# Block 0 of a two-layer transformer: two attention blocks to a group

## The chip, the cores and the metric

The kernel runs on one core of a Trainium2 chip. Its metric is the device time of one execution in microseconds (us); what is quoted is the median of several. A core has engines that run their own queues in program order and meet only at semaphores: TensorE (PE, with its weight loads PEld beside it), VectorE (DVE), ScalarE (ACT), GpSimd (POOL) and SyncE (SP), from whose queue the DMAs of this stage are issued.

## The reference

Two layers work on `x` (8 batches, 512 tokens, 256 channels), a condition (8, 256) and a context (8, 64, 192), all in fp32. The change touches only the first layer:

```python
mod = silu(c) @ adaln_w.T + adaln_b                  # nine rows of 256 per batch
shift_sa, scale_sa, gate_sa, shift_ca, scale_ca, gate_ca, shift_ff, scale_ff, gate_ff = split(mod, 9)
h = modulate(ln(x), shift_sa, scale_sa)              # ln(x) * (1 + scale) + shift
q = ln(heads(h)) * qn_w + qn_b                       # 16 heads of 16; q, k, v all from h
k = ln(heads(h)) * kn_w + kn_b
attn = softmax(q @ k.T * 16 ** -0.5)
x = x + gate_sa * unheads(attn @ heads(h))
h = modulate(ln(x), shift_ca, scale_ca)              # cross attention to 64 tokens
kv = brain_tokens @ cond_w.T + cond_b
...
x = x + gate_ca * (unheads(attn @ v) @ ca_out_w.T + ca_out_b)
h = modulate(ln(x), shift_ff, scale_ff)
x = x + gate_ff * ((silu(h @ w1.T) * (h @ w3.T)) @ w2.T)     # 1024 hidden
```

The second layer has self attention with rotary positions (16 heads of 64), cross attention to the normalized context, and a GELU feed-forward of 1024.

## The kernel before

The first layer is "block 0" of the kernel, the second "block 1". In block 0 each batch goes through three stages, written as the functions `batch1` (self attention), `batch2` (cross attention) and `batch3` (feed-forward).

**Slots and cycles.** The stages are laid out by hand on a row of slots. A cycle has 18 slots (`CYCLE = H + 2`). Sixteen of them hold the attention blocks of one batch in `batch1`: four groups `g` of four heads, by four key tiles `kt` of 128 tokens. Two more (`X0`, `X1`) hold the two blocks of the cross attention of the batch before. A block has two parts. Its scores are four matmuls of 16x512 that work in four row strips of the array and fill two PSUM tiles of two banks each (`bank_s`, of which there are just two); two exponentials of 128x1024 on ACT read them into `p`. Its values are four matmuls in four column strips, `p` against `h`, with a column of ones that gives the softmax denominators.

**What lies beside the slots.** `at(i, fn)` places any other work at slot `i`. `run_blocks` then emits everything: for each slot `i` the scores of block `i`, the values of block `i - 1`, and the work placed at `i`. The order on PE, DVE, ACT and POOL is this order of emission; no scheduler changes it. Cycles are counted from 0. From cycle 2 to cycle 7 three batches are in work: batch b in `batch1`, b-1 in `batch2`, b-2 in `batch3`. The placed work:

- of `batch1`: `norm` in three pieces (statistics of two tiles, of two more, then the layer norm into `ln`, and on POOL `ln` times the scale and plus the shift into `h`), `head_centre`, `head_var` (a square on ACT, a sum on DVE) and `head_scale` (a power and a product on POOL), which make the head norm in the tile `zx` (named `z` in the code); `queries_keys(g)`, four transposes of it, ACT for `q`, DVE for `k`; `group_end(g)`, which copies the values out to `oT`; `group_back(g)`, which transposes oT, divides by the denominators (`den`, `inv`, `attn` on DVE), and for the last group multiplies by the gate and adds to `x` on POOL, 128x1024 each.
- of `batch2`: `prepare(0..2)` (statistics twice, then the layer norm into `z` on DVE and, on POOL, the product `gb` and its addition to `x`), `turn` (eight transposes of `z` and two copies into `hT` on ACT), `queries`, the round trip of the denominators through DRAM (`inverse`, `scaled`), and `project_out` a cycle later.
- of `batch3`: `prepare(0..2)` and `turn` as above, `up(f)` for eight tiles of the hidden layer (four projections each, tanh on ACT, two products on DVE), `down(t)` for four token tiles (eight matmuls on `w_2` each); after every second one a product with the gate and an addition to `x` on DVE, 128x512 (`add_gated`).

PSUM besides the scores' four banks: one bank for values (`ps_O`), and three that `bank_x()` hands out in turn (`ps_X`, `ps_D`) to transposes and projections.

All of the matmuls and transposes but some are issued by helpers, so most PE rows carry one line of the code (109); the tiles' names tell them apart. `ps_S<-q,k` are scores, `ps_O<-p,h` values, `ps_X` or `ps_D<-hT,w` the up projections, `<-w,hid` the down projections, `<-ident,...` transposes, `<-p,vb` and `<-p,sel` the cross attention's values and denominators.

Of the kernel before, what the change touches and what calls it, by code (L numbers as in the profile page):

```python
# [18 lines left out]
P = 128  # L19
# [3 lines left out]
DX = D + HD0  # L23
NPAIR = H // 2
# [19 lines left out]
class Block:  # L44


    def __init__(self, scores, values):
        self.scores, self.values = scores, values
        self.before, self.after = [], []


def run_blocks(blocks, beside=None):


    beside = dict(beside or {})
    for fn in beside.pop(-1, []):
        fn()
    early, late = {}, {}
    for i, bl in enumerate(blocks):
        for lead, fn in bl.before:  # L60
            early.setdefault(max(i - lead, 0), []).append(fn)
        for lag, fn in bl.after:
            late.setdefault(i + 1 + lag, []).append(fn)
    i = 0
    while i <= len(blocks) or any(k >= i for k in (*late, *beside)):
        for fn in early.get(i, []):
            fn()
        if i < len(blocks):
            for fn in blocks[i].scores:
                fn()  # L70
        if 1 <= i <= len(blocks):
            for fn in blocks[i - 1].values:
                fn()
        for fn in (*late.get(i, []), *beside.get(i, [])):
            fn()
        i += 1


def fast_path(ctx: ExitStack, tc: tile.TileContext, a: dict, out: bass.AP):
# [150 lines left out]

    sp_stack = ExitStack()
# [56 lines left out]
    nc.gpsimd.memset(hs[0][:, :, :, HD0 : HD0 + 1], 1.0)  # L288
    nc.gpsimd.memset(sc32, 0.0)
# [189 lines left out]
    X0, X1 = 9, 13  # L479


    def batch1(b):
# [8 lines left out]
        def norm(n):  # L491

            if n == 0:
                s["bc"] = bc = wk.tile([P, 3 * D], F32, tag="bc", name="bc")
                s["h"] = hs[b % 2]
                s["hv"] = s["h"][:, :, :, 0:HD0]
                s["ln"] = wk.tile([P, NT, D], F32, tag="ln", name="ln", bufs=1)
                s["pieces"] = norm_pieces(lambda: s["ln"], xs[b], EPS0)
                if b:
                    spread(bc, b, SH_SA, 3 * D)  # L500
            s["pieces"][n]()
            if b and n == 2:
                ln, bc = s["ln"], s["bc"]
                nc.gpsimd.tensor_tensor(ln, ln, bc[:, None, D : 2 * D].to_broadcast([P, NT, D]), ALU.mult)
                shift = bc[:, 0:D].rearrange("p (h d) -> p h d", d=HD0)
                nc.gpsimd.tensor_tensor(s["hv"], ln.rearrange("p t (h d) -> p t h d", d=HD0),
                                        shift[:, None].to_broadcast([P, NT, H, HD0]), ALU.add)
# [11 lines left out]
        def head_rows():  # L519
            s["z"] = wk.tile([P, NT, DX], F32, tag="zx", name="zx", bufs=1)  # L520
            nc.gpsimd.memset(s["z"][:, :, D if b else 0 : DX], 0.0)

        def head_centre(c, par=None):

            hv = s["hv"][:, :, 8 * c : 8 * c + 8] if par is None else s["hv"][:, :, 8 * c + par : 8 * c + 8 : 2]
            sh = [P, NT, hv.shape[2]]
            mean = small.tile(sh, F32, tag=f"mean{sh[2]}", name="mean", bufs=2)
            nc.vector.tensor_reduce(mean, hv, AX.X, ALU.add)
            nc.vector.tensor_scalar_mul(mean, mean, 1.0 / HD0)
            nc.vector.tensor_tensor(parts(s["z"][:, :, 0:D], c, par), hv,  # L530
                                    mean[:, :, :, None].to_broadcast([*sh, HD0]), ALU.subtract)

        def head_var(c, par=None):
            sq, z = parts(s["ln"], c, par), parts(s["z"][:, :, 0:D], c, par)
            sh = [P, NT, z.shape[2]]
            nc.scalar.activation(sq, z, AF.Square)
            s["var", c, par] = var = small.tile(sh, F32, tag=f"var{sh[2]}", name="var", bufs=2)
            nc.vector.tensor_reduce(var, sq, AX.X, ALU.add)
            nc.vector.tensor_scalar(var, var, 1.0 / HD0, EPS0, ALU.mult, ALU.add)

        def head_scale(c, par=None, eng=None):
            var, z = s["var", c, par], parts(s["z"][:, :, 0:D], c, par)
            n = z.shape[2]
            half = mhalf[:, 0 : NT * n].rearrange("p (t h) -> p t h", t=NT)
            nc.gpsimd.tensor_tensor(var, var, half, ALU.pow)  # L545
            (eng or nc.gpsimd).tensor_tensor(z, z, var[:, :, :, None].to_broadcast([P, NT, n, HD0]), ALU.mult)

        def queries_keys(g):
# [3 lines left out]
            lo = c * P + par * HD0  # L552
            for t in range(NT):
                nc.tensor.transpose(ps[:, t * P : (t + 1) * P], s["z"][:, t, lo : lo + P], ident)  # L554
# [6 lines left out]
        def block(g, kt):  # L561
# [4 lines left out]
            def score():  # L566
# [5 lines left out]
                for u in range(2):  # L572
                    pr[u] = wk.tile([P, 2, N], F32, tag="p", name="p", bufs=4)
                    nc.scalar.activation(pr[u], pss[u], AF.Exp, scale=HD0 ** -0.5)  # L574
# [10 lines left out]
        def group_end(g):  # L585
            oT = wk.tile([P, N], F32, tag="oT", name="oT")
            nc.scalar.copy(oT, s["o", g])  # L587
            s["oT", g] = oT

        def group_back(g):  # L590
            c, par = divmod(g, 2)
            if g == 0:
                s["attn"] = wk.tile([P, NT, D], F32, tag="tok", name="attn", bufs=1)
# [3 lines left out]
            o = s["attn"][:, :, c * P : (c + 1) * P].rearrange("p t (j e d) -> p t j e d", j=4, e=2)[:, :, :, par, :]  # L597
# [5 lines left out]
            nc.vector.tensor_tensor(o, i[:, :, :, 0:HD0], inv[:, :, :, None].to_broadcast([P, NT, 4, HD0]), ALU.mult)  # L603
            check(inv.rearrange("p t j -> p (t j)"))
            if g == 3:
                at_, x = s["attn"], xs[b]
                gate = s["bc"][:, None, 2 * D : 3 * D].to_broadcast([P, NT, D])
                nc.gpsimd.tensor_tensor(at_, at_, gate, ALU.mult)
                nc.gpsimd.tensor_tensor(x, x, at_, ALU.add)

        n = 0
        for g in range(4):
            for kt in range(NT):
# [4 lines left out]
                if g == 0 and kt == 0:  # L618
                    if b == 0:
                        def before():  # L620
                            head_rows()
# [3 lines left out]
                            first_modulated(0, 0)  # L625
                            head_centre(0, 0)
                            head_var(0, 0)
                            head_scale(0, 0, nc.vector)

                        def gate():  # L630
                            spread(s["bc"][:, 2 * D : 3 * D], b, G_SA, D)
# [3 lines left out]
                        at(0, lambda: first_modulated(0, 1))  # L635
                        at(0, lambda: head_centre(0, 1))
                        at(1, lambda: head_var(0, 1))
                        at(1, lambda: head_scale(0, 1))
                        at(2, lambda: first_modulated(1))
                        at(3, lambda: head_centre(1))  # L640
                        at(4, lambda: head_var(1))
                        at(4, lambda: head_scale(1))
                        at(5, gate)
                    else:
                        for m in range(3):
                            at(i - 11 + m, lambda m=m: norm(m))
                        at(i - 6, head_rows)
                        for c in range(2):
                            at(i - 6, lambda c=c: head_centre(c))
                            at(i - 5, lambda c=c: head_var(c))  # L650
                            at(i - 4, lambda c=c: head_scale(c))
                if kt == 0:
                    at(i - 2, lambda g=g: queries_keys(g))
                if kt == NT - 1:
                    at(i + 1, lambda g=g: group_end(g))
                    at(i + 2, lambda g=g: group_back(g))
# [3 lines left out]
    def batch2(b):  # L660
# [27 lines left out]
        def block(c):  # L688
            def score():
# [4 lines left out]
                for u in range(2):  # L694
                    s["p", c, u] = p = wk.tile([P, 2, N], F32, tag="p", name="p", bufs=4)
# [35 lines left out]
        for n in range(3):  # L731
            at(base + 3 + n, lambda n=n: prepare(n))
# [12 lines left out]
    def batch3(b):  # L745
        s = {}

        base = CYCLE * (b + 2) + (3 if b in (B - 3, B - 2) else -2 if b == B - 1 else 0)
# [28 lines left out]
        def down(t):  # L777
            qp, j = divmod(t, 2)
            if j == 0:
                s["ps"] = bank_x()  # L780
            project_tile(s["ps"], j, lambda k: s["hid"][:, k, :], w_2, 8, t)
            if j == 1:
                add_gated(wk2, b, s["gate"])(qp, s["ps"].rearrange("p (j d) -> p j d", j=2))

        for n, i in enumerate((5, 5, 5) if b == B - 1 else (4, 5, 7)):
            at(base + i, lambda n=n: prepare(n))
        later.append((base + 7, turn))
        for f in range(8):
            at(base + 8 + f, lambda f=f: up(f))
        for t in range(4):  # L790
            at(base + 16 + t, lambda t=t: down(t))
# [19 lines left out]
    for t, i in enumerate((10, 11, 14, 15)):  # L811
# [38 lines left out]
    def keys1(p):  # L850
# [3 lines left out]
        kv1[p] = q = kv1["pool"].tile([P, N], F32, tag="q", name="q", bufs=5)  # L854
# [46 lines left out]
    at(CYCLE, open_cross)  # L901
    for p in range(NPAIR):
        at(CYCLE + 4 + p, lambda p=p: keys1(p))
        at(CYCLE + 8 + p, lambda p=p: store_keys1(p))
# [1335 lines left out]
```

## Time and profile before

| what | value |
|---|---|
| time, median of 3 runs | 2450.28 us (2448.86 to 2451.66) |
| time of the profiled execution | 2448.82 us |
| its span, first to last instruction | 2446.9 us |
| granted TensorE clock, mean | 0.997 |
| in one steady cycle (447.8–545.5 us): 32 exponentials of `batch1` on ACT (L574) | 31.0 us |
| there: 48 + 16 up projection matmuls (`ps_X`, `ps_D` <- hT,w) on PE | 22.3 + 7.7 us |
| there: two powers of the head norm (L545) on POOL | 10.9 us |
| whole run: DMA | 84.07 MB, mean 34 GB/s |

The span is the time between the first and the last instruction of one profiled execution; 1.92 us of that execution lie outside it. A row of the timeline has the start in us, the length in us, the engine, the line of the kernel, the operation, the tiles written and read, the shapes and the number of instructions put together in the row; in square brackets the idle time before it and what ended it. In the windows view each row has the window, its length, and for each engine the busy time with the number of instructions in parentheses, then the granted clock, the busy share of the DMA engines and GB/s. The lengths of matmuls are modelled, so where a step's price is wanted it is read from start to start.

### The profile page before, as it was taken

The numbers are of one execution on the slowest core, as the hardware profiler recorded it, in microseconds if no ns is written. First come the engines' busy times: TensorE is split into PE (matmuls) and PEld (weight loads), VectorE is DVE, ScalarE is ACT, GpSimd is POOL, SyncE is SP. The second block draws the span as 40 slices with busy tenths as digits, with TensorE's granted clock in tenths as the row PEclk, the third lists the DMA queues.
The fourth block names the chain that finished last, engine by engine and source line by source line (L and its number), as shares of the span: only waits on it lengthen the run. The fifth ranks groups of instructions, "written<-read, shape, count | busy, mean of one in ns | idle before, by whom it ended". The sixth has DMA issues, their size and how long they took to land.

```text
span 2446.9 us, 28449 instructions
## 1 busy us (share of the span) xinstructions
PE 2408.0 (98%) x10964; PEld 1157.3 (47%) x10964; DVE 1058.9 (43%) x2083; ACT 878.5 (36%) x1118; POOL 858.5 (35%) x538
## 2 busy tenths in 40 slices
PE   9999999999998999999999999999999999999999
PEld 4333443444435643444444444434345555566665
DVE  5544435434434434343434343434334766651210
ACT  4565545545452123333333333333332221222221
POOL 3443222222301026343434343434333444531110
PEclk9999999999999999999999999999999999999999
DMA  5120000000001000000000000000123222210000
GB/s 181 45 93 7 16 20 8 17 11 12 13 11 64 27 1 23 18 19 19 19 18 19 18 19 19 19 18 19 36 61 96 68 67 67 64 55 27 22 18 23
DMA packets 84400, 84.07 MB, mean 34 GB/s; under 512 B 42544, under 2 KB 58784, under 8 KB 84256
## 3 DMA queue, kind: packets, MB, share of 16 engines
q1 hardware_dynamic: 83352, 81.09, 10.6%
q8 instruction: 88, 1.44, 0.2%
q10 hardware_dynamic: 904, 1.07, 0.1%
q14 instruction: 56, 0.46, 0.1%
HBM read 72.09 MB, written 10.04 MB: 34 GB/s over the span
## 4 chain that ended last, share of the span: by engine, by line
PE 92%; DVE 3%; issue 1%; ACT 1%; DMA 1%; POOL 1%; SPq 0%; POOLq 0%; DVEq 0%; ACTq 0%
PE ps_X L109 38%; PE ps_S L109 23%; PE ps_O L109 14%; PE ps_D L109 14%; PE ps_X L416 1%; DVE t L836 1%; DMA rec<-rec 1%; DMA rb<-rec 1%; POOL p L1252 1%; ACT p L574 0%; PE ps_X L554 0%; PE ps_X L596 0%; PE ps_D L416 0%; DVE t L833 0%; ACT hT L417 0%
## 5 line engine op out<-in xcount | busy, mean ns | idle before, releaser
L109 PE MATMUL ps_S<-q,k 32*128 32x512 f32 (+1 forms) x3072 | 429.1, 625 | 7.3 <-ACT p L574 3.1
L1012 ACT ACTIVATE p<-ps_S 128x1024 f32<-128x1024 f32 x256 | 248.1, 1022 | 522.1 <-PE ps_S L109 522.1
L574 ACT ACTIVATE p<-ps_S 128x1024 f32<-128x1024 f32 x256 | 248.2, 1021 | 232.1 <-PE ps_S L109 230.7
L109 PEld LDWEIGHTS ps_S<-q,k 32*128 32x128 f32 (+1 forms) x3072 | 160.5, 184 | 233.1 <-issue 137.5
L991 DVE TENSOR_TENSOR t<-ps_X,rope_c 128x512 f32<-128x512 f32 x126 | 87.2, 692 | 349.9 <-PE ps_X L109 349.9
L1031 DVE TENSOR_TENSOR sm<-sm,p 128x1024 f32<-128x1024 f32 x128 | 190.6, 1532 | 59.2 <-ACT p L1012 59.2
L994 POOL TENSOR_TENSOR q<-t 128x512 f32<-128x512 f32 x32 | 40.8, 1276 | 406.6 <-DVE t L992 406.6
L175 POOL TENSOR_TENSOR rstd<-rstd,mhalf 128x4 f32<-128x4 f32 x49 | 51.0, 1042 | 326.8 <-DVE rstd L174 325.2
L1027 POOL TENSOR_TENSOR sm<-p 128x1024 f32<-128x1024 f32 x64 | 149.3, 2354 | 38.0 <-ACT p L1012 38.0
L109 PE MATMUL ps_X<-hT,w 128*128 128x512 f32 x344 | 160.5, 601 | 1.3 <-ACT hT L417 0.9
L837 POOL TENSOR_TENSOR q<-t,t 128x512 f32<-128x512 f32 x72 | 95.1, 1321 | 176.4 <-DVE t L836 172.4
L109 PE MATMUL ps_O<-p,h 128*32 128x512 f32 x1024 | 139.4, 614 | 1.6 <-ACT oT L587 1.6
L109 PE MATMUL ps_O<-p,v 128*64 128x512 f32 x512 | 138.0, 617 | 0.0
L109 PE MATMUL ps_D<-p,v 128*64 128x512 f32 x512 | 131.6, 592 | 0.0
L453 DVE TENSOR_TENSOR x<-ps_X,x 128x512 f32<-128x512 f32 x27 | 18.7, 692 | 239.4 <-PE ps_X L109 239.4
L109 PE MATMUL ps_X<-hT,w_sa_wq 128*128 128x512 f32 x256 | 115.9, 595 | 3.0 <-ACT hT L417 3.0
L109 PE MATMUL ps_X<-w_sa_wv,hT 128*128 128x512 f32 x256 | 118.0, 604 | 0.0
L109 PE MATMUL ps_X<-w_sa_wo,oT 128*128 128x256 f32 x512 | 114.5, 382 | 0.1
L545 POOL TENSOR_TENSOR var<-var,mhalf 128x32 f32<-128x32 f32 (+1 forms) x17 | 87.3, 5135 | 75.2 <-ACT t L773 41.7
L109 PE MATMUL ps_X<-hT,w_sa_wk 128*128 128x512 f32 x248 | 112.4, 596 | 0.0
L109 PE MATMUL ps_S<-hT,w_ff_w 128*128 128x512 f32 x256 | 111.3, 592 | 0.0
L109 PEld LDWEIGHTS ps_X<-w_sa_wo,oT 128*128 128x128 f32 x512 | 96.0, 190 | 24.2 <-issue 11.4
(282 smaller groups left out, 3537.0 us busy)
## 6 DMA issues: line engine op xcount, KB each, us to landing
rb<-rec SPq DMA_DIRECT2D x128, 128.0 KB
rb<-rec_d SPq DMA_DIRECT2D x124, 128.0 KB
rb<-rec SPq DMA_DIRECT2D x16, 256.0 KB
out_dram<-x SPq DMA_DIRECT2D x15, 256.0 KB
x<-in_x_dram SPq DMA_DIRECT2D x7, 512.0 KB
bc<-modd SPq DMA_DIRECT2D x7, 384.0 KB
gate<-modd SPq DMA_DIRECT2D x16, 128.0 KB
k_d<-q SPq DMA_DIRECT2D x8, 256.0 KB
```

What stands on the lines that cost most here:

```text
L109: nc.tensor.matmul(o, lhsT, rhs, start=start, stop=stop)
L175: nc.gpsimd.tensor_tensor(r[:, :n], r[:, :n], mhalf[:, :n], ALU.pow)
L416: nc.tensor.transpose(ps[:, t * P : (t + 1) * P], z[:, t, k * P : (k + 1) * P], ident)
L545: nc.gpsimd.tensor_tensor(var, var, half, ALU.pow)
L574: nc.scalar.activation(pr[u], pss[u], AF.Exp, scale=HD0 ** -0.5)
L836: nc.vector.tensor_tensor(t2[d], ps[src], sn[src].to_broadcast([64, *shape[1:]]), ALU.mult)
L837: nc.gpsimd.tensor_tensor(dst, t1, t2, ALU.add)
L991: nc.vector.tensor_tensor(c, ps, rope_c, ALU.mult)
L994: nc.gpsimd.tensor_tensor(r[0], ec, os, ALU.subtract)
L1012: nc.scalar.activation(pr, pss[u], AF.Exp, scale=HD1 ** -0.5)
L1027: nc.gpsimd.tensor_tensor(sm, s["p", g, 0, u], s["p", g, 1, u], ALU.add)
L1031: nc.vector.tensor_tensor(s["sm", g, u], s["sm", g, u], s["p", g, t, u], ALU.add)
```

## The change

- `run_blocks` goes by groups of two: for odd `i` the scores of block `i`, the work placed at `i-2` and `i-1`, the scores of block `i+1`, then the values of blocks `i-1` and `i`. So that the cross attention's blocks fall into one group, `X0` goes from slot 9 to 11. The exponential buffers `p` go from four to six, `oT` from two to one.
- The head norm's tile becomes two standing tiles `zs[0]` and `zs[1]`, one for each half of the heads, zeroed once at the start; `head_rows` with its memset per batch is gone. The square is a piece of its own, `head_square`.
- The modulation rows `bc` lose the gate, which gets its own tile and DMA.
- `group_back` multiplies by the gate and adds to `x` for each of the four groups, 128x256 each, in place of one 128x1024 pair for each batch.
- `down(t)` has a half bank, a product and an addition of its own for each `t`, 128x256.
- The placed work moves: `norm` from slots 11, 10, 9 before the batch's first block to 15, 14, 13 before; the head norm's pieces to 11, 9, 7, 7 before for the first half and four later for the second; `queries_keys` from two slots ahead of its group to four (for the group at slot 4 two); `prepare` of `batch2` from 3, 4, 5 to 3, 3, 5; `batch3` by the table `places`, in most batches with `down` at every second slot; some of cycle 0's and cycle 1's setup work by one to four slots.

```diff
-def run_blocks(blocks, beside=None):
...
-    while i <= len(blocks) or any(k >= i for k in (*late, *beside)):
...
-            for fn in blocks[i].scores:
+def run_blocks(blocks, beside):
     for fn in beside.pop(-1, []):
         fn()
+    top = max(len(blocks) + 2, *(k + 3 for k in beside))
+    for i in range(-1, top, 2):
+        for k in (i, i + 1):
+            for fn in blocks[k].scores if 0 <= k < len(blocks) else []:
                 fn()
-        if 1 <= i <= len(blocks):
-            for fn in blocks[i - 1].values:
+            if k == i:
+                for fn in (*beside.get(i - 2, []), *beside.get(i - 1, [])):
+                    fn()
+        for k in (i - 1, i):
+            for fn in blocks[k].values if 0 <= k < len(blocks) else []:
                 fn()
-        for fn in (*late.get(i, []), *beside.get(i, [])):
-            fn()
-        i += 1
...
+    zs = [wk.tile([P, NT, DZ], F32, name=f"z{c}", bufs=1) for c in range(2)]
...
-    X0, X1 = 9, 13
+    X0, X1 = 11, 13
...
-                s["bc"] = bc = wk.tile([P, 3 * D], F32, tag="bc", name="bc")
+                s["gate"] = wk.tile([P, D], F32, tag="gate", name="gate")
...
-                    spread(bc, b, SH_SA, 3 * D)
+                    s["bc"] = bc = wk.tile([P, 2 * D], F32, tag="bc", name="bc", bufs=1)
+                    spread(bc, b, SH_SA, 2 * D)
+                    spread(s["gate"], b, G_SA, D)
...
-        def head_rows():
-            s["z"] = wk.tile([P, NT, DX], F32, tag="zx", name="zx", bufs=1)
-            nc.gpsimd.memset(s["z"][:, :, D if b else 0 : DX], 0.0)
...
+        def head_square(c, par=None):
+            nc.scalar.activation(parts(s["ln"], c, par), head_z(c, par), AF.Square)
...
-                    pr[u] = wk.tile([P, 2, N], F32, tag="p", name="p", bufs=4)
+                    pr[u] = wk.tile([P, 2, N], F32, tag="p", name="p", bufs=6)
...
-            if g == 3:
-                at_, x = s["attn"], xs[b]
-                gate = s["bc"][:, None, 2 * D : 3 * D].to_broadcast([P, NT, D])
-                nc.gpsimd.tensor_tensor(at_, at_, gate, ALU.mult)
-                nc.gpsimd.tensor_tensor(x, x, at_, ALU.add)
+            nc.gpsimd.tensor_tensor(attn, attn, gate.to_broadcast([P, NT, 4, HD0]), ALU.mult)
+            nc.gpsimd.tensor_tensor(x, x, attn, ALU.add)
...
-                        for m in range(3):
-                            at(i - 11 + m, lambda m=m: norm(m))
-                        at(i - 6, head_rows)
+                        for m, k in enumerate((-15, -14, -13)):
+                            at(i + k, lambda m=m: norm(m))
                         for c in range(2):
-                            at(i - 6, lambda c=c: head_centre(c))
-                            at(i - 5, lambda c=c: head_var(c))
-                            at(i - 4, lambda c=c: head_scale(c))
+                            for k, fn in ((-11, head_centre), (-9, head_square), (-7, head_var), (-7, head_scale)):
+                                at(i + k + 4 * c, lambda c=c, fn=fn: fn(c))
                 if kt == 0:
-                    at(i - 2, lambda g=g: queries_keys(g))
+                    at(i - (2 if i == 4 else 4), lambda g=g: queries_keys(g))
                 if kt == NT - 1:
                     at(i + 1, lambda g=g: group_end(g))
-                    at(i + 2, lambda g=g: group_back(g))
+                    at(i + 2 + (n + 1) % 2, lambda g=g: group_back(g))
...
-        for n in range(3):
-            at(base + 3 + n, lambda n=n: prepare(n))
+        for n, i in enumerate((3, 3, 5)):
+            at(base + i, lambda n=n: prepare(n))
         at(base + 6, turn)
...
-        base = CYCLE * (b + 2) + (3 if b in (B - 3, B - 2) else -2 if b == B - 1 else 0)
+        base = CYCLE * (b + 2) + {B - 3: 4, B - 2: 3, B - 1: -2}.get(b, 0)
...
         def down(t):
-            qp, j = divmod(t, 2)
-            if j == 0:
-                s["ps"] = bank_x()
-            project_tile(s["ps"], j, lambda k: s["hid"][:, k, :], w_2, 8, t)
-            if j == 1:
-                add_gated(wk2, b, s["gate"])(qp, s["ps"].rearrange("p (j d) -> p j d", j=2))
+            ps = bank_x()[:, 0:D]
+            project_tile(ps, 0, lambda k: s["hid"][:, k, :], w_2, 8, t)
+            tmp = wk2.tile([P, 2, D], F32, tag="tmp", name="tmp", bufs=1)[:, 0, :]
+            nc.vector.tensor_tensor(tmp, ps, s["gate"], ALU.mult)
+            x = xs[b][:, t, :]
+            nc.vector.tensor_tensor(x, x, tmp, ALU.add)
...
-        for n, i in enumerate((5, 5, 5) if b == B - 1 else (4, 5, 7)):
-            at(base + i, lambda n=n: prepare(n))
-        later.append((base + 7, turn))
+        places = {B - 2: (3, 3, 5, 6, 9), B - 1: (5, 5, 5, 7, 8)}.get(b, (4, 4, 7, 8, 9))
+        for n in range(3):
+            at(base + places[n], lambda n=n: prepare(n))
+        later.append((base + places[3], turn))
         for f in range(8):
-            at(base + 8 + f, lambda f=f: up(f))
+            at(base + places[4] + f, lambda f=f: up(f))
         for t in range(4):
-            at(base + 16 + t, lambda t=t: down(t))
+            at(base + places[4] + 8 + (t if b > B - 3 else 2 * t), lambda t=t: down(t))
```

`spread` issues one DMA from SP's queue that copies modulation rows from DRAM to all partitions; `project_tile` and `project_out` run the matmuls of a projection for one token tile or for two.

## The prediction

> **What bounds the kernel now.** I read the page's busy shares first, then the chain of waits.
>
> ```profile
> PE 2408.0 (98%) x10964; PEld 1157.3 (47%) x10964; DVE 1058.9 (43%) x2083; ACT 878.5 (36%) x1118; POOL 858.5 (35%) x538
> PE 92%; DVE 3%; issue 1%; ACT 1%; DMA 1%; POOL 1%; SPq 0%; POOLq 0%; DVEq 0%; ACTq 0%
> ```
>
> TensorE is never short of work for long: a gain must come out of its own sequence, a loss from anything that makes its queue stand. All edits lie in block 0, which the PE timeline shows at 19–857 us. From one cycle's first scores to the next's it takes 65.9, 72.1 and 95.25 us in cycles 0 to 2, 97.66 in each of 3 to 6, and 120.6 in cycle 7 with its tail. The windows view of one steady cycle, and of a stretch used later:
>
> ```profile
> 447.80:545.50 97.70, 97.40 (x509) 42.62 (x508) 43.76 (x107) 50.08 (x62) 28.76 (x14) 1.00 0.05 14
> 757.00:762.00 5.00, 4.93 (x13) 2.74 (x14) 1.85 (x8) 1.56 (x2) 2.35 (x1) 0.66 0.00 0
> ```
>
> (Length; busy PE, weight loads, DVE, ACT, POOL; granted clock; DMA share.) PE idles 0.3 us of 97.7, yet DVE is busy less than half.
>
> **What grouping gives.** The PE timeline:
>
> ```profile
> 600.79 1.14 PE L109 MATMUL ps_S<-q,k 16*128 16x512 f32 x8
> 601.86 1.06 PE L109 MATMUL ps_O<-p,h 128*32 128x512 f32 x8
> 602.86 1.98 PE L109 MATMUL ps_D<-hT,w 128*128 128x512 f32 x4
> 604.68 1.88 PE L109 MATMUL ps_X<-hT,w 128*128 128x512 f32 x4
> 606.49 1.14 PE L109 MATMUL ps_S<-q,k 16*128 16x512 f32 x8
> ...
> 619.35 1.06 PE L109 MATMUL ps_X<-p,vb 128*32 128x512 f32 x8
> 620.23 1.04 PE L109 MATMUL ps_X<-p,sel 128*32 128x512 f32 x8
> 621.20 0.66 PE L596 MATMUL ps_D<-ident,oT 128*128 128x128 f32 x4
> ```
>
> Start to start, scores take 1.07, values 1.00, a projection pair 3.63. In the middle of a run, eight projection matmuls start 0.427 apart, 3.413 in all; four scores in parallel rows, or four values in parallel columns, are two such passes, 0.853. So leaving scores costs 0.218, values 0.143, projections 0.217. Values behind values (619.35 to 621.20) take 1.85 for 1.707: the change of shape is paid once, 0.147. Two slots paid 2×(0.218+0.143+0.217) = 1.156; a group of scores, beside, scores, two values pays 2×0.218+0.217+0.147 = 0.80, 0.36 less. A steady cycle: 97.66 = 32.4 (18 slots' scores and values) + 6.51 (their exits) + 53.56 (projections and transposes) + 16×0.217 + 1.70 (stalls). After: 32.4 + 53.56 + 18×0.218 + 9×0.147 + 9×0.217 = 93.2.
>
> One stall is new. A block needs both score tiles; its two exponentials start 1.24 us after its scores and take 1.94, so the second tile is free some 3.2 after. Scores that follow two values come 1.07+1.85 = 2.92 after the last ones: 0.29 in 7 of 9 groups. Steady cycle 95.2, −2.45.
>
> **What the new places cost.** Take the group that holds the work of slots 5 and 6, from t7, the transpose of oT behind the scores of slot 7. PE goes on with down(3) on w_2 (3.41), then eight transposes of batch2's z (0.9), and would be at the next scores at t7+4.75. Before, `prepare(2)` wrote z at slot 5, and slot 6's scores and values ran before `turn`; now both are in one group, and in DVE's order z stands behind the multiply and add that need the end of down(3). DVE comes late besides: norm (slots 3, 4, 5), both statistics of `prepare` (3, 3) and `down` are packed into two groups. From t5, the start of down(2) (t7 = t5+8.34), with the DVE timeline's durations:
> - down(2) ends, tmp and x (0.4 each, from attn's 0.42 of the same size): t5+4.4
> - the statistics ending `prepare`: two pairs of 0.75+0.30, overlapped, and rstd, 1.78: 6.2
> - k 0.81, norm's statistics 0.9, `prepare` of batch2 1.78, waits between: t5+10.3 = t7+1.96
> - den, inv, attn, chk 1.1; ln apply 1.4; tmp and x 0.8; z 1.38: t7+6.7.
>
> The last transpose would end at t7+7.05, a wait of 2.3. That is the lower bound, DVE being as fast as it is alone. The POOL and DVE timelines say that it isn't:
>
> ```profile
> 459.72 2.36 POOL L609 TENSOR_TENSOR x<-x,attn 128x1024 f32<-128x1024 f32 x1
> ...
> 478.15 2.37 POOL L437 TENSOR_TENSOR x<-x,gb 128x1024 f32<-128x1024 f32 x1
> ```
>
> ```profile
> 460.48 2.15 DVE L462 TENSOR_TENSOR x<-x,tmp 128x512 f32<-128x512 f32 x1
> ...
> 463.45 0.69 DVE L462 TENSOR_TENSOR x<-x,tmp 128x512 f32<-128x512 f32 x1
> ...
> 476.09 1.38 DVE L208 TENSOR_SCALAR z<-x,mv,rstd 128x256 f32<-128x256 f32 x4
> ...
> 479.42 2.21 DVE L208 TENSOR_SCALAR z<-x,mv,rstd 128x256 f32<-128x256 f32 x4
> ```
>
> The same add is 0.69 alone and 2.15 when it meets a POOL add, and then ends 0.55 after it; z is 1.38 alone, 2.21 beside L437. DVE operations that read PSUM, and statistics, keep their times. In this group POOL now has five operations: attn·gate and x+attn (0.73 each, from the 128x256 gb of L675), ln·scale and h (2.36 each, L504 and L506), gb 0.73. The ln apply, the add and z are held: ln·scale runs from about t7+5.5 to 7.9, the add slips in, h ends at 10.6, one piece of z, gb until 11.4, the rest of z, the transposes: t7+12.75. The wait is 12.75−4.75 = 8.0. Only one more collision, with L437's 2.37, lies above: 10.4. I take 8.0, because the held rows are these very operations. Queued behind: z's transposes on PE, hence the scores of slot 8, their exponentials on ACT, the whole cycle.
>
> Such a wait has a second price:
>
> ```profile
> 757.06 1.44 PE L416 MATMUL ps_D<-ident,z 128*128 128x128 f32 x4 [4.53 <-DVE z L208]
> ```
>
> Behind it, the window 757–762 has clock 0.66, that is 3.41 us at one half, 1.7 lost. I add 1.7 to a wait of 8, nothing to one of 2.3. The Trainium skill's page TensorE: Matmul & The Clock Gate (Part 1, What's actually happening) has the clock halve after an idle window of about 3.4 us and recover after a busy one, the windows running free; by that a wait of 8 could cost 1.7 to 3.4, up to 7 more over four cycles than the sum here.
>
> **Cycle by cycle.**
> - Cycle 0: eight groups at 0.36, less a few 0.29, −2.2. The gaps beyond the exits come to 8.2 today; I let half go, −4.1 (none or all: ±4). But `queries_keys(2)`, at slot 4, now transposes its z in the group in which that z is still squared, summed, raised and scaled; the POOL timeline:
>
> ```profile
> 37.56 5.43 POOL L545 TENSOR_TENSOR var<-var,mhalf 128x32 f32<-128x32 f32 x1 [8.00 <-DVE var L539]
> ```
>
> Exponentials 3.2, square 0.6, var 0.9, power 5.43, product 1.06 (L546) = 11.2, less 1.7 of PE work ahead: 9.5. With the clock's 1.7: +5.
> - Cycle 1: −2.1, a wait of 6 (fewer statistics), clock 1.7: +5.6.
> - Cycle 2: −2.6, short groups +0.9, wait 8, clock 1.7: +8.
> - Cycles 3–6: 4×(−2.45+8.0+1.7) = +29.
> - Cycle 7, without norm: a wait of 1.9, −2.45: −0.5. Tail: the 4.53 falls to 2.4 (−2.1) and its clock loss goes (−1.7), the waits view's 1.2, 1.1 and 0.9 go (−3.1), block 1's first norm now stands before the last hid on DVE (+2.9): −4.
>
> At nothing: the standing z tiles (a 0.15 us memset per batch saved on POOL, idle 65%); exponential buffers, oT, q of kv1 (their users lie slots apart); the adds of `group_back` (5.8 us per batch on POOL for 4.7, beside TensorE; where they meet DVE they are in the 8.0); bc's 384 KB as 256+128, one more issue of 0.32 on SP's queue, now ahead of the softmax round trips: bc is read some 13 us later, and nothing waits for bc today. Were that cover gone, its lateness would move h and add to the same wait.
>
> Sum: 5+5.6+8+29−0.5−4 = +43. The profiled run took 2448.82 (span 2446.9 and 1.9 around it), 1.5 under the median: 2448.8+43 = 2492; I say 2490.
>
> **Rivals.**
> - *The vector chain alone*: POOL's and DVE's pieces interleave without holding each other. For: half of DVE's work here is untouched by POOL today. Against: 460.48, 479.42. Wait 2.3, full clock: cycles 3–6 −0.6, 0 +5, 1 and 2 +0.8, end −4.5: 2449.5. Chance 0.14.
> - *Faster: DVE is in time.* If the statistics fill DVE's waits for down(2) and down(3), z starts right behind down(3)'s add, and PE waits for tmp, x and a first piece, 1.2. Cycles 3–6: 4×(1.2−2.45) = −5; 1 and 2 −1.4; 0 −2, if its z is done some 6 us sooner; end −5.3: 2435. It decides where z begins by t7+5; against it, my 6.7 even without collisions. Chance 0.24: my order of pieces may be off by microseconds.
> - *Pairs save nothing*: exponentials hold the second scores by 0.36 more a pair, so −2.2, −2.1, −2.6 and 5×−2.45 fall away: 2490+19 = 2509. Against it, ACT at 50 of 97.7. Chance 0.05.
>
> **Numbers.** Forecast 0.57, own range 2470 (waits of about 4, no clock loss) to 2506 (10.4). For 8 in 10: 2437 to 2508. A measurement tells 0.2%, 4.9 us, from none: faster 0.22, same 0.10, slower 0.68.
>
> **What would show it.** Right: in each of cycles 2–6 a gap of 6–10 us before transposes of batch2's z, released by DVE's z, clock below 1 behind it, cycles of 103–106; two values in 1.85; some scores 0.3 late. Wrong: cycles below 96 with PE idle under 2, or a gap that DVE's z doesn't end.

## The result and the profile after

The changed kernel takes 2526.8 us (median of 6 runs, 2524.31 to 2529.75) against 2450.2 before: ratio 1.0319, 95% interval 1.0309 to 1.0329. The forecast had the sign; its range for 8 in 10 (2437 to 2508) ended 19 us too low. The page of the changed kernel, busy times and chain:

```profile
PE 2437.1 (96%) x10964; PEld 1185.6 (47%) x10964; DVE 1093.0 (43%) x2115; ACT 880.9 (35%) x1118; POOL 866.4 (34%) x580
PE 88%; DVE 5%; issue 2%; POOL 2%; ACT 1%; DMA 1%; SPq 1%; ACTq 0%; DVEq 0%; POOLq 0%
```

PE has the same 10964 instructions, but span less busy time is 90.4 us instead of 38.9: 51 us more of idleness. And it is busy for 29.1 us longer with the same work, although pairs of blocks were to shorten it: the work ran slower. The windows view, cycles 0 to 2 and one steady cycle (length; busy PE, weight loads, DVE, ACT, POOL; granted clock; DMA share):

```profile
18.90:110.40 91.50, 71.90 (x351) 24.80 (x352) 35.62 (x97) 38.98 (x45) 32.02 (x20) 0.74 0.23 71
110.40:192.50 82.10, 75.05 (x395) 26.86 (x394) 44.03 (x91) 43.27 (x52) 35.38 (x24) 0.88 0.20 63
192.50:296.00 103.50, 94.43 (x440) 35.46 (x440) 47.38 (x109) 51.17 (x63) 35.32 (x22) 0.87 0.11 35
404.20:509.70 105.50, 99.00 (x508) 45.97 (x505) 48.93 (x111) 50.69 (x63) 29.68 (x19) 0.95 0.04 13
```

| stretch | length before, after (us) | change | forecast | PE idle before, after | clock before, after |
|---|---|---|---|---|---|
| cycle 0 | 65.9, 91.5 | +25.6 | +5 | 5.5, 19.6 | 0.97, 0.74 |
| cycle 1 | 72.1, 82.1 | +10.0 | +5.6 | 3.3, 7.1 | 1.00, 0.88 |
| cycle 2 | 95.3, 103.6 | +8.3 | +8 | 0.3, 9.1 | 0.95, 0.87 |
| cycles 3 to 6 | 4 x 97.66, 105.3 to 105.7 | +31.4 | +29 | 0.3, 6.5 each | 1.00, 0.95 |
| cycle 7 and tail, to block 1's first scores | 238.3, 243.0 | +4.7 | -4.5 | 8.4, 7.0 | 0.99, 0.99 |

Idle is a window's length less its PE busy time. Two rows don't compare like with like: in the change `down` ends later, and 32 of its matmuls, some 6.8 us, have gone from cycle 2 (0 for 32 on w_2) to the last row (256 for 224). With the same work cycle 2 is about 15 us longer and the end 2 us shorter.

The steady cycles came as forecast, by the mechanism that was forecast. The PE timeline of one of them, then DVE's and POOL's:

```profile
434.11 0.66 PE L594 MATMUL ps_X<-ident,oT 128*128 128x128 f32 x4
434.60 3.62 PE L100 MATMUL ps_X<-w,hid 128*128 128x256 f32 x16
444.30 0.48 PE L411 MATMUL ps_D<-ident,z 128*128 128x128 f32 x1 [6.08 <-DVE z L199]
...
446.94 2.09 PE L100 MATMUL ps_S<-q,k 16*128 16x512 f32 x8
448.96 3.64 PE L100 MATMUL ps_O<-p,h 128*32 128x512 f32 x16
452.53 1.19 PE L100 MATMUL ps_S<-q,k 16*128 16x512 f32 x8
```

```profile
436.93 2.26 DVE L199 TENSOR_SCALAR ln<-x,mv,rstd 128x256 f32<-128x256 f32 x4
...
439.56 2.33 DVE L772 TENSOR_TENSOR x<-x,tmp 128x256 f32<-128x256 f32 x1
441.81 3.81 DVE L199 TENSOR_SCALAR z<-x,mv,rstd 128x256 f32<-128x256 f32 x4
```

```profile
439.27 2.34 POOL L501 TENSOR_TENSOR ln<-ln,bc 128x1024 f32<-128x1024 f32 x1 [0.55 <-DVE ln L199]
441.69 2.40 POOL L503 TENSOR_TENSOR h<-ln,bc 128x1024 f32<-128x1024 f32 x1
444.05 0.77 POOL L664 TENSOR_TENSOR gb<-gate,rows 128x256 f32<-128x256 f32 x1
```

With t7 = 434.11 the scores stand at t7+12.83, where 12.75 was forecast and 4.75 is what PE's work alone takes. The add, 0.42 alone, ends 0.28 after POOL's first operation; z, 1.38 alone, takes 3.81 through the second and gb. The scores and values behind it then take 2.02 and 3.57 start to start instead of 1.07 and 1.85, since PE's clock is down. In the windows of 3.41 us in which the granted clock moves:

```profile
439.02:442.43 3.41, 0.00 (x0) 0.00 (x0) 3.38 (x4) 0.00 (x0) 3.08 (x2) 1.00 0.13 38
442.43:445.85 3.42, 1.30 (x4) 0.72 (x5) 3.42 (x5) 0.00 (x0) 2.48 (x3) 0.50 0.09 33
445.85:449.26 3.41, 3.41 (x17) 1.47 (x21) 3.34 (x5) 1.69 (x3) 2.26 (x1) 0.50 0.15 49
449.26:452.67 3.41, 3.41 (x20) 0.54 (x12) 0.91 (x3) 1.80 (x2) 0.00 (x0) 0.50 0.00 0
```

One window without work, and three at half follow, two of them with PE busy throughout. The forecast counted one. Cycle 0, where the forecast failed most, on the PE timeline:

```profile
40.25 2.09 PE L100 MATMUL ps_S<-q,k 16*128 16x512 f32 x8 [4.24 <-DVE k L558]
...
57.46 1.12 PE L554 MATMUL ps_D<-ident,z 128*128 128x128 f32 x4 [9.60 <-POOL z L546]
```

The 9.60 is the wait that was forecast (9.5). Beside it stand 4.24 (k of the second group of heads, on DVE behind the modulation and the second half's `head_centre`), 3.58 (at 95.83, the next batch's head norm) and 1.11 (the second scores, for the first exponentials), which were not, and the clock is at half for 47.8 of 91.5 us.

### The profile page after: what moved, and what is told of

It is laid out like the page before. It is cut to its first block, busy times and chain, and to the rows that moved or that the text cites. A ratio compares the mean times of both kernels' runs of the same rounds, so it can differ in the third digit from the quotient of the medians.

```text
span 2527.5 us, 28520 instructions
## 1 busy us (share of the span) xinstructions
PE 2437.1 (96%) x10964; PEld 1185.6 (47%) x10964; DVE 1093.0 (43%) x2115; ACT 880.9 (35%) x1118; POOL 866.4 (34%) x580
## 3 DMA queue, kind: packets, MB, share of 16 engines
q1 hardware_dynamic: 84360, 81.09, 10.4%
q10 hardware_dynamic: 904, 1.07, 0.2%
## 4 chain that ended last, share of the span: by engine, by line
PE 88%; DVE 5%; issue 2%; POOL 2%; ACT 1%; DMA 1%; SPq 1%; ACTq 0%; DVEq 0%; POOLq 0%
PE ps_X L100 35%; PE ps_S L100 22%; PE ps_O L100 14%; PE ps_D L100 13%; PE ps_X L411 1%; DVE z L199 1%; DMA rb<-rec 1%; DVE st L190 1%; DVE ln L199 1%; DVE t L826 1%; POOL var L545 1%; ACT p L574 1%; DVE x L772 0%; POOL p L1242 0%; SPq L1235 0%
## 5 line engine op out<-in xcount | busy, mean ns | idle before, releaser
L100 PE MATMUL ps_S<-q,k 32*128 32x512 f32 (+1 forms) x3072 | 443.7, 642 | 9.5 <-DVE k L558 4.7
L100 PEld LDWEIGHTS ps_S<-q,k 32*128 32x128 f32 (+1 forms) x3072 | 167.6, 190 | 254.1 <-issue 139.0
L100 PE MATMUL ps_X<-hT,w 128*128 128x512 f32 x324 | 148.8, 595 | 0.5 <-DVE t L763 0.5
L100 PE MATMUL ps_O<-p,h 128*32 128x512 f32 x1024 | 144.9, 684 | 0.3 <-ACT oT L587 0.3
L605 POOL TENSOR_TENSOR attn<-attn,gate 128x256 f32<-128x256 f32 x32 | 23.8, 743 | 353.7 <-DVE attn L603 349.6
```

The source lines that it names most:

```text
L100: nc.tensor.matmul(o, lhsT, rhs, start=start, stop=stop)
```

## The experiments

Their times stand beside runs of the kernel before on the same chip (2448.53 to 2451.46 us there, so times are comparable from one to the other to some 3 us).

**Batch2's z earlier, head_centre later.**

```diff
-        for n, i in enumerate((3, 3, 5)):
+        for n, i in enumerate((3, 3, 4)):
...
-                            for k, fn in ((-11, head_centre), (-9, head_square), (-7, head_var), (-7, head_scale)):
+                            for k, fn in ((-9, head_centre), (-9, head_square), (-7, head_var), (-7, head_scale)):
```

> The changed kernel, but batch2's z is written one slot earlier (slot 4, so in the group before its transposes and ahead of the last down's multiply and add), and head_centre goes two slots later (9 before the transposes' group of four instead of 11), so that it doesn't hold batch3's z while it waits for h. Theory 1 (a late z makes PE wait, and the half clock behind it follows from the wait): the 6.3 us gap goes from cycles 1 to 6 and the clock stays at 1 there; steady cycles of 95.0 to 95.6 instead of 105.5; about 2460 in all. Theory 2 (the groups themselves lower the clock, because scores, values and transposes stand together without projections): the gaps go, 39 us in all, but the half-clock stretches stay; steady cycles near 99, about 2488.

2482.58 us against 2448.53, ratio 1.0129 (1.0112 to 1.0146): 44 us less than the change. No PE wait above 1.32 us is left in a steady cycle. The windows view, two steady cycles:

```profile
482.30:580.90 98.60, 96.31 (x510) 45.34 (x506) 48.89 (x111) 50.57 (x63) 29.72 (x19) 1.00 0.05 14
380.60:482.30 101.70, 99.38 (x510) 45.51 (x506) 48.92 (x111) 50.63 (x63) 29.76 (x19) 0.97 0.05 13
```

Three of four cycles keep the full clock and take 98.6, so the half clock of the steady cycles came of the wait. But they aren't the 95.0 to 95.6 of theory 1, and the 99 of theory 2 is met in number only, since it had the half clock stay. Other waits are left: batch3's z ends late (0.50 us), PE waits 0.33 us for DVE's q, and `up` waits 1.3 for a product on DVE, whose tanh stands on ACT behind the square that waits for head_centre. In one cycle the clock falls behind waits as short as these.

**Only z earlier.**

```diff
-        for n, i in enumerate((3, 3, 5)):
+        for n, i in enumerate((3, 3, 4)):
```

> Only batch2's z one slot earlier, head_centre left where the change has it. POOL then adds gb to x (2.35 us) ahead of the norm's scale and shift, h is ready some 3.7 us later, head_centre waits for h on DVE, and batch3's z stands behind it: the wait moves to the next group, about 5 us before the transposes of batch3's z; steady cycles of 102 to 104, about 2515. If nothing stands behind head_centre that PE needs: cycles of 95, about 2460.

2499.74 in one run. The wait did move to batch3's z, with 2.3 us in place of 5, and the clock falls in every steady cycle (100.3 to 101.8 us). Against the run before, head_centre's place is worth 2 us a cycle on the average of the four, 3 where the clock held there.

**Warming matmuls in the wait, 24 and 14.** They work on the identity, and what they write is not read. The diff is that of 24; the second has 14 in its place.

```diff
+        def warm(n):
+            ps = bank_x()
+            for _ in range(n):
+                mm(ps[:, 0:256], ident, chk.rearrange("p i c -> p (i c)"))
+
+        if b < B - 2:
+            at(base + 6, lambda: warm(24))
         at(base + 6, turn)
```

> The changed kernel with 24 matmuls of 128x256 on the identity (no one reads them, some 5.6 us) between the last down and the transposes of batch2's z, for the batches whose transposes lie in cycles 1 to 6: TensorE works through the wait instead of idling, nothing else changes. Theory 1 with the clock as a price of its own: the wait stays in length but the clock stays at 1; steady cycles 4.1 us shorter, 101.4, cycles 1 and 2 shorter by up to 11 and 9; about 2495. Rival (the half clock is hidden, since DVE and ACT set the pace behind the wait): cycles stay at 105, about 2526. If the matmuls reach past the wait, up to 1 us more a cycle.

> As the run with warming matmuls before, but 14 in place of 24: each took 0.43 us there, so 24 filled 10.4 us, 4 more than the wait; 14 fill 6.0. If the half clock has a price of its own, steady cycles of 101.0 to 101.5 at clock 1 in place of 105.5, cycles 1 and 2 as in that run or some 4 us shorter; 2526.8 - 4 x 4.2 - 6 - 6 = about 2498. If DVE and ACT set the pace behind the wait: 105, about 2525.

With 24: 2524.89 against 2448.53. Each is two instructions, 10.4 us in all, so that PE now worked past the wait, and the run told nothing on the price of the clock. With 14: 2509.41 against 2450.09, ratio 1.0237 (1.0222 to 1.0253). Its steady cycle:

```profile
392.70:495.20 102.50, 101.83 (x537) 50.59 (x533) 48.97 (x111) 50.56 (x63) 29.75 (x19) 1.00 0.05 13
```

Clock 1.00, and 102.5 for 105.5, although the transposes still begin 10.3 us behind t7 (10.2 in the change). So in a steady cycle the half clock alone costs 3.0 us, not 1.7; 4 were expected here, and 2498 for the whole.

**POOL's work behind z.**

```diff
-            s["pieces"][n]()
-            if b and n == 2:
-                ln, bc = s["ln"], s["bc"]
+            s["pieces"][n]()
+
+        def norm_shift():
+            if True:
+                ln, bc = s["ln"], s["bc"]
...
+                        at(i - 12, norm_shift)
```

(and head_centre at 9 before.)

> The changed kernel with batch2's z where the change has it (behind the last down's multiply and add), but POOL's two operations on ln (scale, and shift into h, 4.7 us) emitted behind gb and the addition of gb to x, which waits for z; head_centre two slots later. So nothing of POOL but the attention's two short operations and gb meets DVE ahead of z. Theory 1a (z is late because POOL's operations hold DVE's): z starts at once behind the last down's add, the wait before its transposes falls from 6.3 us to between 1.2 and 2.3, the clock stays at 1 in steady cycles; batch3's z may be held in its turn by the operations moved behind it. Rival (z is late because of DVE's own queue): the wait stays above 5.

2512.39 in one run. The DVE and PE timelines, the ln apply, the add, z and the transposes:

```profile
426.22 2.67 DVE L199 TENSOR_SCALAR ln<-x,mv,rstd 128x256 f32<-128x256 f32 x4
...
429.26 0.42 DVE L775 TENSOR_TENSOR x<-x,tmp 128x256 f32<-128x256 f32 x1
429.60 1.38 DVE L199 TENSOR_SCALAR z<-x,mv,rstd 128x256 f32<-128x256 f32 x4
```

```profile
430.06 1.45 PE L411 MATMUL ps_D<-ident,z 128*128 128x128 f32 x4 [2.56 <-DVE z L199]
```

The same operations in the same order on DVE, and with POOL's two elsewhere the add takes 0.42 for 2.33, z 1.38 for 3.81, the wait 2.56 for 6.3 (0.3 more than expected). So it is POOL that makes z late. The 2.56 that remain are near the forecast's lower bound of 2.3, but not by DVE alone: the ln apply, 1.4 alone, meets the attention's two operations of POOL and takes 2.67, so some 1.3 of the 2.56 are POOL's too, by an estimate from these rows. A stretch of 6.8 us at half followed all the same, against the expectation, and the steady cycles take 102.5 to 102.9.

**Cycle 0 alone.**

```diff
-                        at(0, lambda: awake(3))
+                        blocks[0].scores.append(lambda: awake(3))
...
-                        at(2, lambda: head_centre(1))
-                        for k, fn in ((3, head_square), (4, head_var), (4, head_scale)):
-                            at(k, lambda fn=fn: fn(1))
+                        for fn in (first_modulated, head_centre, head_square, head_var, head_scale):
+                            at(2, lambda fn=fn: fn(1))
...
-                    at(i - (2 if i == 4 else 4), lambda g=g: queries_keys(g))
+                    at(i - (3 if i in (4, 8) else 4), lambda g=g: queries_keys(g))
```

> The changed kernel, cycle 0 alone mended: three warming matmuls stand between the first two scores instead of behind them; queries_keys of the second and third group of heads one slot later than the last slot but three (slots 1 and 5), so ahead of the modulation's work on DVE; the second half's head norm starts at slot 2 in one go. Theory (cycle 0 loses 28 us to three waits, 9.6, 4.2 and 1.1, and to the half clock that follows them): gaps of at most 4 in all in the first 60 us, half clock there for under 15 us instead of 37; cycle 0 shorter by 15 to 25, about 2507. Rival (cycle 0 is bound by the chain of the head norm on DVE and POOL, wherever its parts stand): the gap moves to the next transposes, under 8 us gained.

2509.24 against 2448.53, ratio 1.0241 (1.0223 to 1.0258): time and clock as the theory had them, while the gaps of the first 60 us come to about 5 in place of at most 4. The windows view, cycle 0:

```profile
19.50:87.80 68.30, 58.94 (x348) 22.49 (x348) 34.73 (x97) 38.67 (x45) 31.96 (x20) 0.95 0.27 87
```

68.3 for 91.5 us, with clock 0.95 for 0.74 and 9.4 idle for 19.6. Of the 23.2 gained some 10 are waits; the rest is the clock.

**All mends, with pairs and slot by slot.** To the edits above come head_centre at 10 before, batch 1's power two slots earlier, gb and its addition to x in a piece of their own, and the first norm of block 1 a slot later; the second kernel goes slot by slot as the kernel before does:

```diff
-            if n < 2:
-                return
-            gate = s["gate"]
+
+        def gate_bias():
+            gate = s["gate"]
...
+        at(base + 8, gate_bias)
...
-    at(CYCLE * (B + 1) + 1, first_norm)
+    at(CYCLE * (B + 1) + 2, first_norm)
```

> The mends together: cycle 0 as in the run on it; batch2's z one slot earlier; gb and its addition to x four slots later, on their own, so that they no longer hold the layer norm of batch1 and batch3's z; head_centre one slot later than in the change; the power of batch 1's first half two slots earlier; block 1's first norm one slot later. From 2482.6 (steady mend): cycle 0 -23, each steady cycle 98.6 to 96 or less (-10), cycle 7's tail -4: about 2445, a tie with the kernel before or up to 0.3% faster. If the groups lower the clock by themselves, half-clock stretches remain where only scores, values and transposes stand (cycles 1 and 2), and it stays above 2450.

> The kernel with all mends, but emitted slot by slot as before the change (scores of i, values of i-1, the work at i), so that the pairs alone are taken away. If a pair saves 0.36 us less 0.29 in 7 of 9 groups, a steady cycle is longer by 1.2 to 2.8 us than with pairs (sections 4.46 - 1.70 - 2.03 at the least, 3.2 without waits for exponentials), about +15 in all. If the pairs lower the clock in cycles 0 to 2, single slots lose less there, or win.

2458.09 with pairs (ratio 1.0031, 1.0019 to 1.0043) and 2455.99 slot by slot (1.0026, 1.0017 to 1.0036), against 2450.09. Both expectations missed: the tie didn't come, and the pairs seemed worth nothing. The windows view of a steady cycle in which the clock held, with pairs and then slot by slot:

```profile
357.20:455.00 97.80, 95.59 (x508) 45.32 (x504) 49.31 (x111) 50.63 (x63) 29.93 (x19) 1.00 0.05 14
354.00:452.40 98.40, 97.65 (x505) 42.37 (x504) 50.26 (x111) 49.74 (x62) 29.94 (x19) 1.00 0.05 14
```

The two kernels differ only in the order of emission, so the pairs do save: 2.06 us of PE's busy time. But PE idles 2.2 for 0.75, and cycle 1 takes 77.2 us with pairs and 68.6 without. The trace with pairs shows where the idle time comes from, DVE's and POOL's rows:

```profile
396.24 5.94 DVE L199 TENSOR_SCALAR z<-x,mv,rstd 128x256 f32<-128x256 f32 x4
```

```profile
396.11 2.43 POOL L503 TENSOR_TENSOR h<-ln,bc 128x1024 f32<-128x1024 f32 x1
398.49 0.79 POOL L662 TENSOR_TENSOR gb<-gate,rows 128x256 f32<-128x256 f32 x1
399.36 2.34 POOL L432 TENSOR_TENSOR x<-x,gb 128x1024 f32<-128x1024 f32 x1
```

Four slots later in the program, gb and its addition started as soon as POOL was free, ran straight on behind h, and the three together held batch3's z, which takes 1.38 alone, for 5.94: PE waited 1.7 in each steady cycle. A place in POOL's order isn't a time.

**Behind an operation that waits; pairs only where projections stand between.** The first edit is in both kernels, the second (slot by slot up to slot 36) in one.

```diff
-        at(base + 8, gate_bias)
+        at(base + 12, gate_bias)
...
+    for i in range(37):
+        for fn in (*blocks[i].scores, *(blocks[i - 1].values if i else []), *beside.pop(i, [])):
+            fn()
-    for i in range(-1, top, 2):
+    for i in range(37, top, 2):
```

> All mends, with gb and its addition to x at slot 12 (behind an operation of POOL that waits for the next group's values, so that they meet neither z), slot by slot in cycles 0 and 1 (slots 0 to 36), in pairs from there on. From the two runs before: cycle 0 66.5 and cycle 1 68.6 as with single slots, steady cycles of 95.2 to 96.2 at clock 1 as the pairs' sections give, 2458 - 3 - 9 - 4 x 3 = about 2434, faster than the kernel before by 0.5 to 0.8%. If the pairs' saving doesn't come (steady cycles stay near 98), about 2444.

> The same with pairs from the first slot on, as the change has it. The difference to the run before is what the pairs cost in cycles 0 and 1, where few projections stand between them: 12 us if the clock falls there as in the run with all mends (13.7 + 3.4 us at half with no wait above 0.6 us ahead of it), 2446; none if that clock fell for the waits alone.

2431.0 us with single slots in cycles 0 and 1, 2438.57 with pairs throughout, against 2451.46: ratios 0.9918 (0.9904 to 0.9931) and 0.9956 (0.9941 to 0.9971). Both are faster than the kernel before, the first by 0.8%. The windows view of the first, cycle 1 and a steady cycle, and then of the second:

```profile
85.20:153.70 68.50, 67.17 (x385) 22.29 (x384) 39.94 (x93) 43.26 (x52) 34.92 (x25) 1.00 0.25 81
342.70:438.00 95.30, 95.13 (x508) 45.26 (x504) 48.03 (x111) 50.62 (x63) 29.89 (x19) 1.00 0.05 14
```

```profile
82.80:160.60 77.80, 74.73 (x393) 25.99 (x392) 40.88 (x91) 43.42 (x52) 32.55 (x24) 0.89 0.19 59
444.90:540.20 95.30, 95.13 (x510) 45.27 (x506) 48.03 (x111) 50.56 (x63) 29.87 (x19) 1.00 0.05 14
```

A steady cycle is 95.3 in both: 97.66 less 2.36, where the forecast's sections gave 95.2. Cycle 1 is 9.3 us longer with pairs than with single slots: clock 0.89 for 1.00 and 3.1 idle for 1.3. Cycle 0 is 3.2 shorter with pairs, in part because work of it falls into cycle 1. Over cycles 0 to 2, which hold the same matmuls in both, pairs cost 6.1 us (231.7 for 225.6), and over the whole run 7.6, not 12.

## Where the prediction was right and where it failed

- *What grouping gives* was right: 2.45 forecast for a steady cycle, 2.36 measured once nothing else stood in the way. That it comes of the pairs is shown by the two kernels with all mends, 2.06 us of busy time with nothing but the order changed.
- *The group of slots 5 and 6* was right in place, cause and size: 8.0 forecast, 8.08 measured from PE's own 4.75 to the scores. Some 0.5 of these is already the clock's, since with 14 matmuls in the wait the scores stand at t7+12.29. The cause is shown by the run with POOL's work elsewhere. With it the rival "vector chain alone" falls, and so does "DVE is in time", which needed z to begin by t7+5: it began at t7+7.7, and at t7+6.2 even in that run.
- *The waits of cycles 1, 2 and 7* were near: 5.6 for 6 (2.70, 1.88, 0.80, 0.26), 8.0 for 8, 1.3 for 1.9. In the tail z's wait fell to 1.95 (2.4 forecast) and the first norm's became 3.15 (2.9), but the 3.41 us at half stayed. That cycle 2 as a whole came out at +8.3 for +8 is luck: its clock loss was larger than forecast, and some 6.8 us of `down`, which the forecast left in place, went to the end.
- *"Such a wait has a second price … I add 1.7"* is the step that failed, as a term that was mis-sized. The granted clock was at half for 139.9 us in place of 17.1. Halving PE's busy time in these stretches gives at most 56.9 us lost against 8.2: 49 more (some 17 in cycle 0, 8 in cycle 1, 7 in cycle 2 and 16 in cycles 3 to 6), where the forecast had seven times 1.7, less 1.7. In steady cycles the run with 14 matmuls gives 3.0 for one such wait. That lies within the 1.7 to 3.4 which the prediction estimated from the Trainium skill's page TensorE: Matmul & The Clock Gate (Part 1, What's actually happening), although in the change the clock was at half for three windows around each such wait. And "nothing to one of 2.3" failed with it: in the run with POOL's work elsewhere a wait of 2.56 was followed by 6.8 us at half. The kernel before had shown it. The forecast took its price from 757–762 alone, but at the end of cycle 1 a wait of 2.09 came with 10.2 us at half, with at most 4.8 us lost; the PE timeline and the windows view of before:

```profile
157.23 2.09 PE L109 MATMUL ps_S<-q,k 16*128 16x512 f32 x8 [2.09 <-DVE k L558]
```

```profile
155.00:160.00 5.00, 2.91 (x16) 0.75 (x16) 2.05 (x5) 1.77 (x3) 3.81 (x2) 0.67 0.13 36
160.00:164.00 4.00, 4.00 (x20) 0.98 (x16) 0.69 (x1) 2.54 (x4) 0.00 (x0) 0.50 0.19 70
164.00:168.00 4.00, 4.00 (x19) 2.50 (x12) 1.00 (x5) 1.24 (x2) 0.58 (x1) 0.64 0.00 0
```

- *Cycle 0* failed by its list too. It priced the one wait that was found at 9.5 for 9.60, and of the others it said "I let half go" of today's gaps: there were 8.9 us in three further waits, and the kernel before has none at their places. The k of 4.24 now stands in one group with the scores that need it, the power behind the 3.58 stands in the group just before its transposes, and the 1.11 is between two scores that had warming matmuls between them. With the clock behind them cycle 0 has 21 of the 38 us by which the sum was short.
- The covers held otherwise: nothing waits for bc, gate or oT's buffer in the trace of the change.

So the 80.6 us by which the profiled span grew are about 51 of waiting and up to 49 of half clock, less a remainder of some 20, near the 19 that the forecast had for the pairs.

## What to carry to other kernels

Before operations are gathered into larger groups, list for each group every pair of producer and consumer that comes to lie in the same one, and not only the first that is found. Where POOL and DVE both work from SBUF to SBUF, give the long POOL operations a place where an earlier one in their queue must wait, for a later slot alone doesn't move them. Price a wait of TensorE together with the clock that it loses, and from more than one such wait in the trace. Look at the clock before grouping everywhere: here pairs kept it at 1.00 in steady cycles, where projections stand in most groups, and had 0.89 for 1.00 in cycle 1, where few do.

## What the runs showed of the hardware

The clock fell without a wait. In the change, at the end of cycle 1, this window has PE busy for 3.40 of 3.41 us:

```profile
189.85:193.26 3.41, 3.40 (x20) 1.31 (x16) 1.09 (x6) 2.71 (x3) 0.00 (x0) 1.00 1.03 411
```

The window after it ran at half, as the PE timeline shows by the two values in it (195.38 to the next scores at 198.96, 3.58 for 1.85):

```profile
190.15 1.71 PE L100 MATMUL ps_S<-q,k 16*128 16x512 f32 x8
191.79 0.66 PE L594 MATMUL ps_D<-ident,oT 128*128 128x128 f32 x4
192.46 2.99 PE L100 MATMUL ps_S<-q,k 16*128 16x512 f32 x8
195.38 3.64 PE L100 MATMUL ps_O<-p,h 128*32 128x512 f32 x16
198.96 1.67 PE L100 MATMUL ps_S<-q,k 16*128 16x512 f32 x8
```

The first window held 2.44 us of scores, 0.66 of transposes, 0.30 of values, and no projection. The Trainium skill's TensorE: Matmul & The Clock Gate (Part 1, What's actually happening) speaks of an idle window; here a busy one was enough. Nor did one busy window bring the clock back: it stayed at half through 445.85 to 452.67, two windows with PE busy throughout, and in cycle 0, behind the wait of 9.60, through three (60.14 to 70.38), the first of them with little but projections. Scores fill 16 rows in each of four strips of the array; that the clock's control takes such matmuls for little activity would fit the fall, but was not tried by itself, and why the clock came back so late stays open. The four runs with z earlier and head_centre later lie 10 us apart, with mean clocks of 0.982 to 0.987, the slowest with the lowest; what sets the one or the other is not shown.
